# Edge loop of a graph network: three engines issue in text order, and a dense unit's result stands ahead of the next unit's first transposes

## The chip, the cores and the metric

The kernel runs on one core of one Trainium2 chip. A core has a matrix engine (PE, with its weight loads PEld), a vector engine (DVE), a scalar engine (ACT), a general engine (POOL) that here issues the indirect gathers, and a queue engine (SP) that issues the other transfers. Each engine takes its instructions in the order in which the program hands them over, and waits on semaphores for the others. Sixteen DMA engines serve the core. The metric is device time in microseconds for one execution; a single core runs, so its time is the time.

## The reference

Two graph networks follow each other over the same 3125 nodes and 100,000 edges (`src`, `dst`, sorted by `dst` in the drawn inputs). The first has four layers of attention over the incoming edges of a node, with 8 heads of 16:

```python
q = (h @ Wq.T + bq)[dst].reshape(-1, HEADS, D_HEAD)
k = (h @ Wk.T + bk)[src].reshape(-1, HEADS, D_HEAD)
v = (h @ Wv.T + bv)[src].reshape(-1, HEADS, D_HEAD)
alpha = jnp.sum(q * k, axis=-1) / float(np.sqrt(D_HEAD))
amax = jax.ops.segment_max(alpha, dst, num_segments=n)
ex = jnp.exp(alpha - amax[dst])
denom = jax.ops.segment_sum(ex, dst, num_segments=n)
a = ex / (denom[dst] + 1e-16)
out = jax.ops.segment_sum((a[:, :, None] * v).reshape(-1, f), dst, num_segments=n)
...
beta = jax.nn.sigmoid(jnp.concatenate([out, x_r, out - x_r], axis=-1) @ Wbeta.T)
return beta * x_r + (1.0 - beta) * out
```

After each attention come a layer norm and a two-layer GELU network with residuals. The second network sums one message per edge into its node and updates the nodes; the change does not touch it.

## The kernel before

Edges are sorted by target and cut into chunks of 128 that stay within one tile of 128 nodes. A group `g` is 4 chunks (512 edges). Nodes of the first 4 tiles (`DT`) have so many edges that their attention is done densely, as a matrix over all nodes with a mask of edge counts; the other nodes' edges go through the edge loop in 123 groups (`SPG`). So one layer runs two things interleaved in one loop, `edge_sums`.

**Edge steps.** `rows_of(g)` gathers the group's k and v rows into one of 5 `kvg` buffers (4 indirect DMAs, issued by POOL, L690). `fetch` loads (layers 1 to 3) the one-hot rows that layer 0 built and stored; `one_hot` builds them in layer 0 (L674). `select` multiplies them on PE with q (L754, `q_ps`, two buffers). `scores` multiplies by k and reduces to `alpha` on DVE (L766, L767). `values` copies v out of `kvg` on ACT (L776). `weights` scales v by the exponentials on DVE (L793) and, in layer 0, builds one-hot columns (L681). `by_node` sums over a node's edges on PE (L808, `s_ps`, one buffer until the last 8 groups), and `add` adds that to the accumulators on DVE (L824).

**Turns.** Turn `g` of the loop runs, in the text, `rows_of(g+4)`, `fetch(g+3)`, `add(g-14)`, `one_hot(g+2)`, dense slots, one step of `mixing` if due, `scores(g)`, `select(g+1)`, `advance()`, dense slots, `values(g)`, `advance()`, `columns(g-11)`, `weights(g-12)`, `advance()`, `by_node(g-13)`. `LAG` is 12: the exponentials need the maxima of a batch of 8 groups (`GB`). From turn -3 to 136, a layer has 140 turns.

**Maxima.** `Maxima.steps` is a generator that takes one batch's `alpha` through transposes on PE (`m_ps`, L585, L564, L554, L634), copies and scans on DVE (L591, L566, L594 to L598, L557, L600, L604, L612, L614, L618) and copies and exponentials on ACT (L587, L628 to L638). Each `advance()` runs it up to its next `yield`; the first three pieces fall into the turn of the batch's last group, b=7, the next three into the turn after. Pieces 3 to 6 each end with a PE transpose of what DVE has just made in the same piece:

```python
yield from self.row(top[:, 0:1], back[:, :, :IB])
```

**Dense steps.** `dense_steps` cuts the dense attention into 16 units (4 tiles, 4 pairs of heads) and 258 slots of 15 a unit; `due(at, count, step)` places a step of unit `u` in the slots from `15u + at` on. A unit computes scores chunk by chunk (`scores`, L897, `d_ps`, one buffer), adds the mask and takes the maximum on DVE (`masked`, L907), takes exponentials on ACT (`exps`, L920, 14 of them), transposes on PE into `pt_ps`, one buffer (`turn`, L929), copies that out on ACT (`turned`, L936), and multiplies by v on PE (`weigh`, L946, `av`). After every fourth unit `result` copies `av` out (L951), transposes it through `pt_ps` (L954) and adds two halves on ACT and DVE (L959, L960). `others` runs 14 slots in the first turn and then 1.92 slots a turn. Within a slot the text has `weigh`, `scores`, `turned`, `exps`, `turn`, `masked`, `maxima`, `result`.

**What sets the order.** In the kernel before, the program's framework orders the instructions of every engine itself: it walks a model of their times and takes those whose inputs are there, the earlier in the text first. Buffers of a pool go round in the order of the text, and a new user waits until the last one has been read.

**Mixing.** When a block of 4 node tiles is complete, 9 steps of `mixing` (L1100 to L1146) are popped one a turn, four blocks a layer.

Of the kernel before, what the change touches and what calls it, by code (L numbers as in the profile page):

```python
# [14 lines left out]
ET = mybir.EngineType  # L15
# [851 lines left out]
PAIRS = [(0, 2), (1, 3), (4, 6), (5, 7)]  # L867
# [3 lines left out]
def dense_steps(tc, k, s, a, keep, work, ps):  # L871

    nc = tc.nc
    v, kt, qz = a["v"], a["kt"], a["qz"]
    chunks = [(c, min(NS, NT - c)) for c in range(0, NT, NS)]
    units = [(d, pair) for d in range(DT) for pair in PAIRS]
    live = {}  # L880
    dense = keep.tile([P, DT, HEADS, DX], F32, name="dense")

    av = ps.tile([P, len(PAIRS), P], F32, name="av", bufs=1)
    nc.vector.memset(av, 0.0)

    def scores(u, j):
        d, pair = units[u]
        c, n = chunks[j]
        if j == 0:
            live[u] = dict(mx=work.tile([P, 2, len(chunks)], F32, name="mx"), sm=[], s_ps={},  # L890
                           t_ps={}, pt={})
        mask = work.tile([P, NS * P], F32, name="mask", bufs=2)
        nc.sync.dma_start(mask[:, :n * P], s["mask_d"][d, :, c * P:(c + n) * P])
        s_ps = [ps.tile([P, NS * P], F32, name=f"d_ps{i}", bufs=1) for i in range(2)]
        for i, h in enumerate(pair):
            r = slice(h // 2 * 32, h // 2 * 32 + 32)
            nc.tensor.matmul(s_ps[i][:, :n * P], qz[r, h % 2, d * P:(d + 1) * P],  # L897
                             kt[r, c * P:(c + n) * P], start=True, stop=True)
        live[u]["s_ps"][j] = s_ps, mask

    def masked(u, j):
        n = chunks[j][1]
        s_ps, mask = live[u]["s_ps"].pop(j)
        sm = work.tile([P, 2, NS * P], F32, name="sm", bufs=9)
        live[u]["sm"].append(sm)
        for i in range(2):
            nc.vector.tensor_tensor_reduce(  # L907
                out=sm[:, i, :n * P], in0=s_ps[i][:, :n * P], in1=mask[:, :n * P], scale=1.0,
                scalar=-3.0e38, op0=ALU.add, op1=ALU.max, accum_out=live[u]["mx"][:, i, j:j + 1])

    def maxima(u):
        top = work.tile([P, 2], F32, name="dtop")
        nc.vector.tensor_reduce(top, live[u]["mx"], axis=AX.X, op=ALU.max)
        nc.vector.tensor_scalar(top, top, -1e20, -1.0 / DH ** 0.5, op0=ALU.max, op1=ALU.mult)  # L914
        live[u]["top"] = top

    def exps(u, j, i):
        n = chunks[j][1]
        sm = live[u]["sm"][j]
        nc.scalar.activation(sm[:, i, :n * P], sm[:, i, :n * P], AF.Exp,  # L920
                             scale=1.0 / DH ** 0.5, bias=live[u]["top"][:, i:i + 1])

    def turn(u, i):
        t_ps = ps.tile([P, 2, 2, P], F32, name="pt_ps", bufs=1)
        for x in range(min(2, NT - 2 * i)):
            t = 2 * i + x
            sm = live[u]["sm"][t // NS]
            for y in range(2):
                nc.tensor.transpose(t_ps[:, x, y, :], sm[:, y, t % NS * P:(t % NS + 1) * P],  # L929
                                    k.ident)  # L930
        live[u]["t_ps"][i] = t_ps

    def turned(u, i):
        n = min(2, NT - 2 * i)
        pt = work.tile([P, 2, 2, P], F32, name="pt")
        nc.scalar.copy(pt[:, :n], live[u]["t_ps"].pop(i)[:, :n])  # L936
        live[u]["pt"][i] = pt

    def weigh(u, i):
        d, pair = units[u]  # L940
        pt = live[u]["pt"].pop(i)
        for x in range(min(2, NT - 2 * i)):
            t = 2 * i + x
            for y, h in enumerate(pair):
                r = (2 * x + y) * 32
                nc.tensor.matmul(av[r:r + DX, u % len(PAIRS), :], v[:, t, h, :], pt[:, x, y, :],  # L946
                                 start=(i == 0), stop=(t + 2 >= NT))

    def result(d):
        out = work.tile([P, len(PAIRS), P], F32, name="dout", bufs=1)  # L950
        nc.scalar.copy(out, av)  # L951
        t_ps = ps.tile([P, len(PAIRS), 2, 2, 32], F32, name="pt_ps", bufs=1)
        for j in range(len(PAIRS)):
            nc.tensor.transpose(t_ps[:, j].rearrange("p x y d -> p (x y d)"), out[:, j, :],  # L954
                                k.ident)

        o = dense[:, d].rearrange("p (a y b) d -> p a b y d", a=2, b=2)
        for a_ in range(2):
            nc.scalar.copy(o[:, a_], t_ps[:, 2 * a_:2 * a_ + 2, 0, :, :DX])  # L959
            nc.vector.tensor_add(o[:, a_], o[:, a_], t_ps[:, 2 * a_:2 * a_ + 2, 1, :, :DX])  # L960

    NH = (NT + 1) // 2
    NC_ = len(chunks)

    def slot(i):

        def due(at, count, step):

            u, j = divmod(i - at, 15)
            if 0 <= u < len(units) and j < count:  # L970
                step(u, j)

        due(19, NH, weigh)
        due(0, 2 * NC_, lambda u, j: scores(u, j // 2) if j % 2 == 0 else None)
        due(18, NH, turned)
        due(15, 2 * NC_, lambda u, j: exps(u, j // 2, j % 2))
        due(17, NH, turn)
        due(1, 2 * NC_, lambda u, j: masked(u, j // 2) if j % 2 == 0 else None)
        due(14, 1, lambda u, j: maxima(u))
        due(19 + NH, 1, lambda u, j: result(units[u][0]) if u % len(PAIRS) == len(PAIRS) - 1  # L980
            else None)
        due(19 + NH, 1, lambda u, j: live.pop(u))

    return dense, [lambda i=i: slot(i) for i in range(15 * (len(units) - 1) + 20 + NH)]


# [169 lines left out]
def attention(tc, k, s, a, l):  # L1156


    nc = tc.nc
    nc.gpsimd.memset(a["acc"], 0.0)  # L1160

    def pools(name, groups, dense):
        with tc.tile_pool(name=name + "k", bufs=1) as keep, \
                tc.tile_pool(name=name + "w", bufs=2) as work, \
                tc.tile_pool(name=name + "m", bufs=1) as mw, \
                tc.tile_pool(name=name + "p", bufs=1, space=PSUM) as ps:
            if dense:

                early = [(upto * IC // GC + LAG + 2, step) for b, upto in DONE.items()
                         for step in mixing(tc, l, a, mw, b)]  # L1170
                sums, beside = dense_steps(tc, k, s, a, keep, work, ps)
                edge_sums(tc, k, s, a, groups, beside, early, "load" if l else "store", keep,
                          work, ps, ps)

                nc.vector.tensor_copy(a["acc"][:, :DT], sums)
            else:
                edge_sums(tc, k, s, a, groups, [], [(groups + LAG + 2, step) for b in DONE
                                                    for step in mixing(tc, l, a, mw, b)],
                          None, keep, work, ps, ps)

    with tc.If(s["general"] == 0) as arm:
        pools("some", SPG, True)
    with arm.Else():
        pools("all", NG, False)
# [597 lines left out]
```

## Time and profile before

| What | us |
|---|---|
| runs | 4689.97, 4687.6, 4693.14 (median 4689.97) |
| the profiled execution | 4700.52 |
| its span, first to last instruction | 4698.7 |
| edge loop of layer 0 | 350 to 1112 |
| edge loop of layer 1 | 1206 to 1913 |
| edge loop of layer 2 | 2009 to 2718 |
| edge loop of layer 3 | 2812 to 3523 |
| second network | about 3600 to the end |

In the page, the 40 slices show the loops as the stretches in which PE, DVE and POOL are all high:

```profile
PE   3757999887799989879989888998987666667775
DVE  5765989986478888548878854887875444445643
...
POOL 2014777760477776047777514777742777777775
PEclk9666989898789999969999996999998888888887
```

Each digit is a tenth of busy time in a slice of 117 us, the last row the granted clock of PE. A group's line in the page names the source line, the engine, the tiles it writes and reads, its count, its busy time and mean, and then the idle time of the engine just before it and what ended most of that:

```profile
L936 ACT COPY pt<-pt_ps 128x512 f32<-128x512 f32 (+1 forms) x832 | 471.4, 567 | 804.0 <-PE pt_ps L929 796.5
L920 ACT ACTIVATE sm<-sm,dtop 128x512 f32<-128x512 f32 (+1 forms) x896 | 539.8, 668 | 14.9 <-DVE dtop L914 14.1
```

ACT has much idle time; an instruction there is seldom late for want of the engine, but those behind a long run of others wait for it.

### The profile page before, as it was taken

What the parts mean: (1) busy time and instruction counts of PE and PEld (TensorE: products, weight loads), DVE (VectorE), ACT (ScalarE), POOL (GpSimd) and SP (SyncE); (2) the same over time, 40 slices, a digit from 0 to 9 for tenths busy, and PEclk for the clock granted to TensorE, in tenths of its full rate; (3) what the DMA queues carried; (4) which work ended last, traced back from release to release, by engine and by line L of the source; (5) the groups of instructions that cost most, each with busy time, mean ns of one, the idle gap of its engine ahead of it and who ended that gap; (6) DMA issues with size and microseconds to landing.
All of it is one profiled execution on the core that took longest, in us unless ns stands there. A gap on an engine that the chain in (4) does not pass through costs nothing. (4 is left out here: it accounts for less than half of the span.)

```text
span 4698.7 us, 84645 instructions
## 1 busy us (share of the span) xinstructions
PE 3820.5 (81%) x25947; PEld 2695.1 (57%) x25947; DVE 3205.5 (68%) x9975; ACT 2183.8 (46%) x4470; POOL 2808.9 (60%) x2821
## 2 busy tenths in 40 slices
PE   3757999887799989879989888998987666667775
PEld 1324666664466666546666644666664665656664
DVE  5765989986478888548878854887875444445643
ACT  2873555454256555535555543555544323332331
POOL 2014777760477776047777514777742777777775
PEclk9666989898789999969999996999998888888887
DMA  2125888882578778357877735787862333334332
GB/s 58 40 96 174 270 251 266 243 230 76 180 218 261 246 242 226 98 167 242 261 240 247 193 113 173 245 262 231 253 178 60 93 93 90 91 90 87 97 90 52
DMA packets 449718, 801.31 MB, mean 171 GB/s; under 512 B 91381, under 2 KB 173830, under 8 KB 449184
## 3 DMA queue, kind: packets, MB, share of 16 engines
q1 hardware_dynamic: 327040, 481.12, 31.7%
q0 software_dynamic: 121392, 313.35, 25.6%
q8 instruction: 229, 3.75, 0.3%
q14 instruction: 273, 2.24, 0.2%
q10 hardware_dynamic: 784, 0.85, 0.1%
HBM read 693.94 MB, written 102.26 MB: 169 GB/s over the span
## 5 line engine op out<-in xcount | busy, mean ns | idle before, releaser
L690 POOL DMA_INDIRECT kvg<-kv_d,src_i x1968 | 1967.7, 1000 | 1086.3 <-issue 620.1
L690 POOL DMA_INDIRECT ag<-a_d,src_i x816 | 794.5, 974 | 255.3 <-issue 222.7
L936 ACT COPY pt<-pt_ps 128x512 f32<-128x512 f32 (+1 forms) x832 | 471.4, 567 | 804.0 <-PE pt_ps L929 796.5
L907 DVE CUSTOM_DVE_ANT_0 sm<-d_ps,mask 128x512 f32<-128x512 f32 (+1 forms) x896 | 542.1, 625 | 230.5 <-PE d_ps L897 132.3
L897 PE MATMUL d_ps<-kt,qz 32*128 32x512 f32 (+1 forms) x1792 | 603.2, 659 | 47.9 <-DVE mx L907 42.0
L929 PE MATMUL pt_ps<-ident,sm 128*128 128x128 f32 x3200 | 572.4, 301 | 74.5 <-ACT pt L936 48.1
L754 PE MATMUL q_ps<-q,hrows 128*128 x3936 | 611.0, 301 | 12.1 <-issue 6.5
L929 PEld LDWEIGHTS pt_ps<-ident,sm 128*128 128x128 f32 x3200 | 366.5, 149 | 401.1 <-issue 207.2
L754 PEld LDWEIGHTS q_ps<-q,hrows 128*128 128x128 f32 x3936 | 543.0, 212 | 88.7 <-issue 63.5
L808 PE MATMUL s_ps<-ev,hcols 128*128 128x136 f32 x3744 | 567.4, 295 | 16.4 <-DVE acc L824 7.6
L920 ACT ACTIVATE sm<-sm,dtop 128x512 f32<-128x512 f32 (+1 forms) x896 | 539.8, 668 | 14.9 <-DVE dtop L914 14.1
L808 PEld LDWEIGHTS s_ps<-ev,hcols 128*128 128x128 f32 x3744 | 500.2, 200 | 45.2 <-issue 23.7
L776 ACT COPY ev<-kvg 128x512 f32<-128x512 f32 x492 | 302.7, 617 | 439.7 <-DMA kvg<-kv_d,src_i 260.5
L1567 PE MATMUL s_ps<-m,hcols 128*128 128x129 f32 x1632 | 278.1, 323 | 258.4 <-DVE acc L1576 236.7
L1567 PEld LDWEIGHTS s_ps<-m,hcols 128*128 128x128 f32 x1632 | 248.0, 230 | 294.6 <-ACT m L1560 166.2
L1559 DVE TENSOR_TENSOR m<-ag,m_ps 128x512 f32<-128x512 f32 x204 | 139.7, 687 | 393.5 <-DMA ag<-a_d,src_i 353.9
L766 DVE TENSOR_TENSOR qk<-q_ps,kvg 128x512 f32<-128x512 f32 x492 | 336.1, 683 | 100.8 <-PE q_ps L754 88.0
L946 PE MATMUL av<-pt,v 128*17 128x128 f32 x6400 | 367.5, 286 | 0.7 <-ACT pt L936 0.7
L793 DVE TENSOR_TENSOR ev<-ev,ex 128x512 f32<-128x512 f32 x492 | 333.3, 682 | 7.5 <-ACT ex L638 7.2
L767 DVE TENSOR_REDUCE alpha<-qk 128x32 f32<-128x512 f32 x492 | 333.0, 677 | 3.2
L1560 ACT ACTIVATE m<-m 128x512 f32<-128x512 f32 x204 | 125.1, 627 | 436.4 <-DVE m L1559 430.7
L824 DVE TENSOR_TENSOR acc<-acc,s_ps 128x136 f32 x936 | 266.8, 285 | 40.1 <-PE s_ps L808 31.5
(324 smaller groups left out, 5180.1 us busy)
## 6 DMA issues: line engine op xcount, KB each, us to landing
mask<-mask_d SPq DMA_DIRECT2D x384, 256.0 KB
hrows<-hrows_d SPq DMA_DIRECT2D x369, 256.0 KB
hcols<-hcols_d SPq DMA_DIRECT2D x369, 256.0 KB
hrow<-drow_d SPq DMA_DIRECT2D x327, 128.0 KB
kvg<-kv_d,src_i POOLq DMA_INDIRECT x1968
hrows_d<-hrows SPq DMA_DIRECT2D x123, 256.0 KB
hcols_d<-hcols SPq DMA_DIRECT2D x123, 256.0 KB
ag<-a_d,src_i POOLq DMA_INDIRECT x816
```

Source lines behind the costliest of these rows:

```text
L690: nc.gpsimd.indirect_dma_start(out=out[:, x, :], out_offset=None, in_=table[:], in_offset=bass.IndirectOffsetOnAxis(ap=s["src_i"][:, i:i + ...
L754: nc.tensor.matmul(qs[g][:, x, :], hot[:, c * P:(c + 1) * P], a["q"][:, bass.ds(tn["PE"][item_of(g, c)], 1), :], start=True, stop=True)
L766: nc.vector.tensor_mul(qk, qs.pop(g), kvg[:, :, :HID])
L793: nc.vector.tensor_mul(e[:, :, :, :DH], e[:, :, :, :DH], ex.unsqueeze(3).to_broadcast([P, IC, GH, DH]))
L808: nc.tensor.matmul(sums[g][:, c // IC], hot[:, c, :], ev[:, ORDER.index(c)].rearrange("p h d -> p (h d)"), start=(c % IC == 0), stop=(c % ...
L897: nc.tensor.matmul(s_ps[i][:, :n * P], qz[r, h % 2, d * P:(d + 1) * P], kt[r, c * P:(c + n) * P], start=True, stop=True)
L907: nc.vector.tensor_tensor_reduce(out=sm[:, i, :n * P], in0=s_ps[i][:, :n * P], in1=mask[:, :n * P], scale=1.0, scalar=-3.0e38, op0=ALU.add ...
L920: nc.scalar.activation(sm[:, i, :n * P], sm[:, i, :n * P], AF.Exp, scale=1.0 / DH ** 0.5, bias=live[u]["top"][:, i:i + 1])
L929: nc.tensor.transpose(t_ps[:, x, y, :], sm[:, y, t % NS * P:(t % NS + 1) * P], k.ident)
L936: nc.scalar.copy(pt[:, :n], live[u]["t_ps"].pop(i)[:, :n])
L946: nc.tensor.matmul(av[r:r + DX, u % len(PAIRS), :], v[:, t, h, :], pt[:, x, y, :], start=(i == 0), stop=(t + 2 >= NT))
L1567: nc.tensor.matmul(s_ps[:, c // IC, :], h[:, c, :], x[:, c, :], start=(c % IC == 0), stop=(c % IC == IC - 1))
```

## The change

Two edits. The edge loop is wrapped so that PE, ACT and DVE keep the order of the text; POOL and SP are still ordered by the framework. And in a slot, `result` now stands before `turn`.

```diff
@@ dense_steps, slot
         due(15, 2 * NC_, lambda u, j: exps(u, j // 2, j % 2))
+        due(19 + NH, 1, lambda u, j: result(units[u][0]) if u % len(PAIRS) == len(PAIRS) - 1
+            else None)
         due(17, NH, turn)
         due(1, 2 * NC_, lambda u, j: masked(u, j // 2) if j % 2 == 0 else None)
         due(14, 1, lambda u, j: maxima(u))
-        due(19 + NH, 1, lambda u, j: result(units[u][0]) if u % len(PAIRS) == len(PAIRS) - 1
-            else None)
         due(19 + NH, 1, lambda u, j: live.pop(u))
@@ attention, pools
                 sums, beside = dense_steps(tc, k, s, a, keep, work, ps)
-                edge_sums(tc, k, s, a, groups, beside, early, "load" if l else "store", keep,
-                          work, ps, ps)
+
+                with tc.manual_schedule(engines={ET.PE, ET.Activation, ET.DVE}):
+                    edge_sums(tc, k, s, a, groups, beside, early, "load" if l else "store", keep,
+                              work, ps, ps)
```

`result` of unit `u` falls into slot 15u + 32, which is also the slot of the first `turn` of unit `u + 1`; both use the one buffer of `pt_ps`. In the text before, `turn(u+1, 0)` would take that buffer first and its copy, `turned(u+1, 0)`, comes in the next slot, behind `result`. In the new text `result` writes and frees it before `turn` does. No instruction is added or taken away.

## The prediction

> **What bounds the kernel now.** First the page's span and engine rows, then the busy time by stage, then the timelines of single batches.
>
> ```profile
> span 4698.7 us, 84645 instructions
> PE 3820.5 (81%) x25947; PEld 2695.1 (57%) x25947; DVE 3205.5 (68%) x9975; ACT 2183.8 (46%) x4470; POOL 2808.9 (60%) x2821
> L690 POOL DMA_INDIRECT kvg<-kv_d,src_i x1968 | 1967.7, 1000 | 1086.3 <-issue 620.1
> ```
>
> The change touches the four edge loops (first d_ps product to last addition: 350 to 1112, 1206 to 1913, 2009 to 2718, 2812 to 3523), 2888 of the 4699 us. The busy time by stage of layer 1 (columns: stretch, length, then busy time and instructions of PE, PEld, DVE, ACT, POOL, granted clock, DMA share, GB/s); the last row is the same part of layer 0.
>
> ```profile
> 1219.00:1283.50 64.50, 49.65 (x228) 28.05 (x227) 24.48 (x66) 19.99 (x34) 29.18 (x31) 0.62 0.50 153
> 1328.30:1861.50 533.20, 496.37 (x4159) 350.56 (x4159) 447.66 (x1323) 300.06 (x644) 406.37 (x412) 0.96 0.80 247
> 1413.80:1451.00 37.20, 36.57 (x321) 26.06 (x321) 32.81 (x93) 22.94 (x51) 28.36 (x30) 1.00 0.84 265
> 1565.00:1613.10 48.10, 41.26 (x323) 29.06 (x321) 33.77 (x93) 24.69 (x54) 36.52 (x39) 0.89 0.73 230
> 427.20:1044.70 617.50, 561.34 (x4454) 391.03 (x4454) 558.41 (x1595) 325.10 (x694) 468.46 (x446) 0.91 0.83 251
> ```
>
> Row 2 is the steady part, turns 15 to 119: 13 batches of 8 turns, 41.0 us each. PE is busy 93%. POOL has a floor: a gather takes 0.95 us and the next follows 0.30 later, so the 32 of a batch need 40.0 us. Little is left to win there: (41.0-40.0) x 13 = 13 us a layer. Row 3 is a good batch: PE has no gap and the clock is full. Row 4 is a bad one, and the timelines of PE and ACT show why:
>
> ```profile
> 1567.23 0.39 PE L946 MATMUL av<-pt,v 128*17 128x128 f32 x2
> 1574.46 0.37 PE L564 MATMUL m_ps<-ident,fwd 128*1 128x128 f32 x1 [6.84 <-DVE fwd L591]
> 1575.31 2.08 PE L754 MATMUL q_ps<-q,hrows 128*128 x8
> ```
> ```profile
> 1567.24 6.20 ACT L920 ACTIVATE sm<-sm,dtop 128x512 f32<-128x512 f32 x11
> 1573.34 0.35 ACT L587 COPY at<-m_ps 128x256 f32<-128x256 f32 x1
> ```
>
> ACT was given 11 exponentials of a dense unit ahead of the copy that the edge maxima wait for; PE stood for 6.84 us and then ran at half clock (2.08 for a q product of 1.06). By the waits of PE in row 2's stretch, L564 waits for DVE fwd 28.0 us in 9 waits. Over the batches of layers 1 to 3, length minus PE gaps minus half of the half-clock time is 35 to 40, mean 36.6 us: PE's own work.
>
> **The change, part by part.** Nothing is added or removed but order: PE, ACT and DVE now follow the text; SP and POOL don't. Outside the maxima turns PE's order is already the text's (av, d, T, q, av, T, s; starts 0.35, 1.06, 0.49, 0.99, 0.35, 0.49, 1.02 us apart), so a plain turn costs the same. Three things change.
>
> (a) *The exponentials are spread, one a slot.* The 6.8 us gap and its like go. Cleared of gaps and slow clock a batch is 36.6.
>
> (b) *PE now waits at the maxima steps.* In turns b=7, +1 and +2 of every batch, advance() puts a DVE step and the PE transpose that needs it side by side, five times; the trace moves those transposes behind the next s, av and d, the text doesn't. DVE's turn starts when PE ends the turn before (add needs the last s_ps). DVE steps, start to start: two adds 0.65, qk+alpha 1.32, a masked pair 1.25, ev 0.61, forward scan 0.66, backward 0.65, small copies and scan 0.90. Walk from a turn's start at 0, scores in the first slot. Turn b=7: alpha is done at 2.0, PE's alpha transpose goes at 2.9 unhindered; DVE's masked pair and ev end at 3.9, ACT's copy at 4.1, fwd at 4.8; PE arrived at 4.05: 0.95 lost. Next turn: rows are ready at 2.9, PE there at 2.9: 0.2 with the hand-over; then masked, col, fwd, back to 5.55, PE there at 4.1: 1.6; then ev, copy, scan, copy to 6.95, PE there at 6.0: 1.15. Third turn: sub at 3.2, gains, ACT's exponential at 4.35, PE there at 3.73: 0.8. Sum 4.7. With scores in the second slot the masked pair comes before qk: 1.6 + 2.5 + 0.85 + 1.5 = 6.45. Parity flips at every 15-slot unit: mean 5.5 us a batch (4 to 8). Behind the waiting transpose stand s, av, d and T on PE, and DVE's next add and ACT's next pt copy wait for those. The 28 mixing steps a layer (1.4 to 2 us of DVE) fall for 3/8 into these turns: 28 x 3/8 x 1.6 = 17, over 14 batches 1.0 with a little for the others (0 to 1.6).
>
> Half clock after gaps: in layer 1 a gap of 2.06 us at 1826.89 was followed by d, T, q of 1.40, 1.11, 1.92 (granted clock 0.67 over 4 us), one of 2.35 at 1747.75 by none (1.00). New gaps are 0.2 to 2.5 us; I take 0.8 us a batch (0 to 3). [...]
>
> Steady batch: 36.6 + 5.5 + 1.0 + 0.8 = 43.9 against 41.0: +2.9 x 13 = +38 us a layer. POOL (40) isn't the bound then. Layer 0 computes one-hots: hot_rows and hot_cols add 0.9 us of DVE to each maxima turn, some 1.2 of it seen by PE a batch. 37.2 (same way) + 6.7 + 1.0 + 0.8 = 45.7 against (1044.7-472.0)/13 = 44.0 (starts of the q products of turns 119 and 15): +22.
>
> (c) *The start.* From the first d_ps product (1206.5) to the q product of turn 15 (1328.3) it takes 121.8 us; row 1 shows PE at clock 0.62. ACT ran 13 exponentials in a row (1250.80, 7.75 us), T waited 5.8 and 4.0, by its timeline POOL stood 28 us more than in its rhythm from 1222 to 1300. In the text all 7 chunks of unit 0 come first: first masked pair ends at 1214.9 as now, then six rounds of 2.08 (cold d) + 1.31 + 0.2, the last short: 1235. Then turns without s_ps: two cold ones of 6, eleven of 3.7, two of 4.7, one batch of maxima with 7.6: about 1304. Gain 24 us (5 to 35), all layers.
>
> (d) *The dense result ahead of turn.* turn(u+1,0) shares pt_ps, one buffer: PE now waits for dout (0.58, behind one exponential of 0.67), four transposes (0.61), two copies and two additions of 0.2 with hand-overs, before its T: 2.3 us (0 to 3.5), 4 a layer: +9. It issues no DMA; behind it stand T, q or s on PE and the masked pair on DVE, which it now precedes. Before, T was already issued and s covered the transposes (1424.59).
>
> (e) *Tail*, turn 119 to the last addition, 51.5 us now: ten turns of add, ev, s of 1.6, the rest as above: +2 (-5 to +8). SP's and POOL's own order may shift; PE waited 0.6 us for hrows in row 2's stretch, so I take 0.
>
> Layers 1 to 3: 38-24+9+2 = +25 each, 75; layer 0: 22-24+9+2 = +9. **Sum +84**. The profiled execution took 4700.5 us (span 4698.7): 4784.5, 1.8% more. Against the median 4690.0: **4774 us**.
>
> **Rivals.** *The covers hold (faster).* If PE reaches each transpose late enough (as in the good batch), or DVE runs ahead, batches stay at 41.0, result costs nothing, the start's 24 us are won: -22 x 4 = -88, 4602; with all batches at POOL's 40.0 (DVE's busy time in layer 0, 558.4/14 = 39.9, allows it) (13+24) x 3 + (52+24) = 187 less, 4503. For: row 3, and the bursts of exponentials surely go. Against: the walk finds PE early at five steps.
>
> *Half clock in every batch (slower still).* If the new gaps put PE at half clock for most of each maxima stretch, 3 us more a batch, so 46.9: layers 1 to 3 +64 each, layer 0 +48, total +240: 4930. For: the start stays at 0.62 with gaps of only 0.4 to 0.8 us between 1225 and 1243. Against: the 2.35 us gap left 1.00. It decides from gaps of about 2 us in each 3 to 4 us window.
>
> *Nothing happens.* The order is the text's in most turns already; gains at the start and losses in the batches cancel: within 10 us of 4690. This is just +64 in the batches eaten by a better start.
>
> **Chances.** Forecast 0.50 (own range 4705 to 4860), faster 0.25, half clock 0.17, nothing 0.08. The range 4605 to 4910 leaves out half of the faster case and somewhat over half of the half-clock one, 0.2 in all. A measurement of this kernel tells about 0.2% (9 us) from no change: faster 0.25, same 0.08, slower 0.67.
>
> **What would show it.** Right: no run of more than 3 exponentials on ACT in a row; waits of L564, L554 and L634 on PE of 0.5 to 2.5 us, four or five a batch, some 75 us a layer where row 2 had 34; the start over 20 us shorter; L954 followed by a wait of about 2 us at T. Wrong: batches of 41 or less, PE gaps under 3 us a batch, or POOL at its 1.25 us rhythm without a break: then the text hides the round trips and it is faster. Clock under 0.9 in the steady part: the half-clock case.

## The result, and the profile after

| | before | after |
|---|---|---|
| median, us | 4688.78 (4685.03 to 4693.14) | 5023.46 (5017.87 to 5034.8) |
| ratio to before, 95% interval | | 1.0718 (1.07 to 1.0736) |
| profiled execution, us | 4700.52 | 5022.12 |
| its span, us | 4698.7 | 5020.3 |

The change makes the kernel 7.2% slower. The direction was forecast, the size was not: +84 us of span were predicted and +322 came, beyond the forecast's 4605 to 4910.

The page after, first its span, the busy time of the engines and PE's granted clock in 40 slices, then one group (busy time, mean ns of one, idle time before it and what ended most of it):

```profile
span 5020.3 us, 84716 instructions
...
PE 3931.7 (78%) x25947; PEld 2802.8 (56%) x25947; DVE 3369.9 (67%) x9975; ACT 2156.9 (43%) x4470; POOL 2794.8 (56%) x2821
...
PEclk7658888887888888888888888888888788888887
...
L824 DVE TENSOR_TENSOR acc<-acc,s_ps 128x136 f32 x936 | 276.4, 295 | 479.5 <-PE s_ps L808 455.1
```

The counts of PE and DVE are those of before, and yet PE was busy 111 us longer with them: the same instructions ran more slowly, at a mean granted clock of 0.830 (0.871 before). (DVE's 164 us more were not followed up.) The clock row had nines in the four loops before; now it stays at 8. The last line is new among the costly ones. In the page of before it reads:

```profile
L824 DVE TENSOR_TENSOR acc<-acc,s_ps 128x136 f32 x936 | 266.8, 285 | 40.1 <-PE s_ps L808 31.5
```

DVE's first step of a turn, the addition, now waits 455 us for PE's last step of the turn before; it used to wait 31.5. PE and DVE go in lockstep.

Stages of the kernel after, from the busy time by stretch (length, then PE, PEld, DVE, ACT, POOL with instructions, granted clock, DMA share, GB/s). In order: steady part of layer 1 (turns 15 to 119), one batch of it, steady part of layer 0, start of layer 1, its tail:

```profile
1394.20:2020.40 626.20, 536.66 (x4160) 380.36 (x4159) 474.57 (x1316) 292.95 (x642) 417.69 (x424) 0.86 0.70 213
1532.40:1578.20 45.80, 40.44 (x327) 28.78 (x327) 34.60 (x94) 22.39 (x50) 31.93 (x33) 0.89 0.75 224
...
444.80:1128.10 683.30, 558.54 (x4159) 394.31 (x4158) 575.53 (x1523) 293.71 (x642) 426.83 (x417) 0.85 0.72 214
1306.10:1394.20 88.10, 75.64 (x502) 45.77 (x502) 54.26 (x141) 39.45 (x72) 50.20 (x53) 0.81 0.72 220
2020.40:2087.00 66.60, 45.09 (x332) 35.13 (x330) 47.26 (x147) 22.36 (x60) 2.99 (x4) 0.82 0.38 80
```

A steady batch took 626.2 / 13 = 48.2 us where it took 41.0. The start of the layer is indeed shorter (121.8 us before), and its clock is 0.81 where the start before had 0.66 (0.62 in the stretch that the prediction shows).

Cut in the same way, every layer says the same. *Start* runs from the first d_ps product to the q product of turn 15, *steady* from there to that of turn 119, *tail* to the last addition. *Gaps* are the idle stretches of PE over 0.1 us in the steady part, *half clock* the time in it for which the trace grants PE about half its clock.

| us | start | steady | tail | gaps | half clock |
|---|---|---|---|---|---|
| before, layer 0 | 121.5 | 572.7 | 67.1 | 51.2 | 85.3 |
| before, layer 1 | 121.8 | 533.2 | 51.1 | 36.6 | 44.4 |
| before, layer 2 | 121.7 | 533.3 | 54.2 | 37.7 | 41.0 |
| before, layer 3 | 121.9 | 537.1 | 51.8 | 39.8 | 44.4 |
| after, layer 0 | 97.3 | 683.3 | 84.7 | 124.7 | 211.6 |
| after, layer 1 | 88.2 | 626.2 | 66.7 | 89.3 | 177.5 |
| after, layer 2 | 88.1 | 625.5 | 67.0 | 89.8 | 174.1 |
| after, layer 3 | 88.7 | 628.9 | 66.8 | 87.6 | 187.7 |

The four loops grew by 104, 75, 71 and 74 us, 324 in all: the whole difference of the spans (322).

The waits of PE in the steady part of layer 1 (waiting line, releaser: us in total, times, longest):

```profile
PE m_ps L554 <- DVE rows L598: 26.8, 13, 4.9
PE m_ps L554 <- DVE into L614: 18.0, 13, 1.5
PE m_ps L564 <- DVE back L609: 12.2, 7, 2.2
PE m_ps L585 <- DVE alpha L767: 8.4, 5, 3.1
PE m_ps L564 <- DVE fwd L591: 7.0, 8, 1.4
PE m_ps L634 <- ACT at L628: 3.5, 6, 1.7
```

Two of these, `rows` and `into`, occur 13 times, once in every batch. The maxima transposes are the places, as the walk said. L554, L564 and L634 come to 70 us with the smaller rows, where "some 75 us a layer" had been forecast; L585 adds 8. One second maxima turn, on PE and then on DVE (start, duration, and in brackets the idle time before and what ended it):

```profile
1490.23 1.16 PE L754 MATMUL q_ps<-q,hrows 128*128 x8
1492.12 0.19 PE L554 MATMUL m_ps<-ident,into 1*128 1x1 f32 x1 [0.73 <-DVE rows L598]
1492.24 0.40 PE L946 MATMUL av<-pt,v 128*17 128x128 f32 x4
1494.85 0.37 PE L564 MATMUL m_ps<-ident,top 128*1 128x128 f32 x1 [2.21 <-DVE back L609]
1496.59 0.23 PE L554 MATMUL m_ps<-ident,into 1*128 1x1 f32 x1 [1.36 <-DVE into L614]
1496.75 2.18 PE L808 MATMUL s_ps<-ev,hcols 128*128 128x136 f32 x8
1498.86 2.08 PE L897 MATMUL d_ps<-kt,qz 32*128 32x512 f32 x4
```

```profile
1488.94 0.63 DVE L824 TENSOR_TENSOR acc<-acc,s_ps 128x136 f32 x2 [1.29 <-PE s_ps L808]
...
1496.18 0.26 DVE L614 COPY into<-back 1x120 f32<-1x120 f32 x1
1498.97 0.63 DVE L824 TENSOR_TENSOR acc<-acc,s_ps 128x136 f32 x2 [2.53 <-PE s_ps L808]
1502.27 0.23 DVE L960 TENSOR_TENSOR dense<-dense,pt_ps 128x68 f32<-128x68 f32 x1 [2.67 <-ACT dense L959]
```

The walk had 0.2, 1.6 and 1.15 us for these three waits of PE; they were 0.73, 2.21 and 1.36. After them the products s and d take 2.18 and 2.08 us at a granted clock of 0.50 (1.09 and 1.13 at 1.00, from 1535.37 on), and DVE's next addition waits 2.53 us for that slow s. Behind the gaps stands a second loss, at half clock, and DVE passes it into the next turn, which begins with that addition.

### The profile page after: what moved, and what is told of

It reads as the page before. It is cut to its first block, busy times and chain, and to the rows that moved or that the text cites. A ratio compares the mean times of both kernels' runs of the same rounds, so it can differ in the third digit from the quotient of the medians.

```text
span 5020.3 us, 84716 instructions
## 1 busy us (share of the span) xinstructions
PE 3931.7 (78%) x25947; PEld 2802.8 (56%) x25947; DVE 3369.9 (67%) x9975; ACT 2156.9 (43%) x4470; POOL 2794.8 (56%) x2821
## 5 line engine op out<-in xcount | busy, mean ns | idle before, releaser
L920 ACT ACTIVATE sm<-sm,dtop 128x512 f32<-128x512 f32 (+1 forms) x896 | 600.8, 677 | 114.1 <-DVE dtop L914 114.1
L808 PE MATMUL s_ps<-ev,hcols 128*128 128x136 f32 x3744 | 625.3, 319 | 10.2 <-DVE bs L1135 3.1
L897 PE MATMUL d_ps<-kt,qz 32*128 32x512 f32 (+1 forms) x1792 | 589.3, 701 | 38.6 <-DVE mx L907 32.6
L754 PE MATMUL q_ps<-q,hrows 128*128 x3936 | 600.8, 303 | 21.9 <-DVE acc L824 3.5
L929 PE MATMUL pt_ps<-ident,sm 128*128 128x128 f32 x3200 | 588.8, 310 | 31.1 <-ACT pt L936 17.2
L929 PEld LDWEIGHTS pt_ps<-ident,sm 128*128 128x128 f32 x3200 | 380.7, 154 | 395.1 <-issue 251.7
L907 DVE CUSTOM_DVE_ANT_0 sm<-d_ps,mask 128x512 f32<-128x512 f32 (+1 forms) x896 | 528.3, 626 | 91.7 <-PE d_ps L897 64.9
L808 PEld LDWEIGHTS s_ps<-ev,hcols 128*128 128x128 f32 x3744 | 556.8, 222 | 26.8 <-issue 13.1
```

The source lines that it names most:

```text
L754: nc.tensor.matmul(qs[g][:, x, :], hot[:, c * P:(c + 1) * P], a["q"][:, bass.ds(tn["PE"][item_of(g, c)], 1), :], start=True, stop=True)
L808: nc.tensor.matmul(sums[g][:, c // IC], hot[:, c, :], ev[:, ORDER.index(c)].rearrange("p h d -> p (h d)"), start=(c % IC == 0), stop=(c % ...
L907: nc.vector.tensor_tensor_reduce(out=sm[:, i, :n * P], in0=s_ps[i][:, :n * P], in1=mask[:, :n * P], scale=1.0, scalar=-3.0e38, op0=ALU.add ...
```

## The experiments

All ratios are to before. The start, steady and tail times and the gaps are read as in the table. For each kernel that keeps the text order, the comparison is with after.

**The result's move alone.** The text order is taken away.

```diff
-                with tc.manual_schedule(engines={ET.PE, ET.Activation, ET.DVE}):
+                if True:
```

> Only the moved result; the three engines are ordered by the framework as before. If the order of the text is the whole cause, this is the kernel before again: 4680 to 4700 us (ratio 0.998 to 1.003), steady batches of layer 1 at 41 us, clock 0.96 there. If the result ahead of turn costs the 2.3 us each that the prediction gave it, 16 of them add up to 37 us: 4725.

4699.5 us, ratio 1.0005 (0.999 to 1.0019). The move by itself costs nothing that can be measured; layer 1 has 36.1 us of gaps and 51.2 of half clock, near before's 36.6 and 44.4. All of the 7.2% comes with the text order.

**ACT alone in the order of the text.**

```diff
-                with tc.manual_schedule(engines={ET.PE, ET.Activation, ET.DVE}):
+                with tc.manual_schedule(engines={ET.Activation}):
```

> Only ACT keeps the order of the text; PE and DVE are ordered by the framework. If the runs of 11 to 13 exponentials on ACT are what cost the kernel before its long PE gaps, they go and nothing else gets worse: no wait of PE for fwd over 3 us, steady batches at 38 to 40 us, 4560 to 4640. If pacing ACT costs as much elsewhere (PE waits for pt copies that stand behind a late exponential), 4680 to 4760.

4682.8 us, ratio 0.9963 (0.9947 to 0.9979): slightly faster, and less so than expected. The starts are 11 to 20 us shorter, the steady parts of layers 1 to 3 gain 9.5, 3.0 and 6.2 us, and the tails lose 12 to 18; layer 0's steady part lost 9.4. The long waits did shrink: PE's wait for `fwd` in the steady part of layer 1 fell from 28.0 to 13.8 us. But spreading the exponentials is worth little in the batches, because they then meet the gathers: layer 1's batch is 523.7 / 13 = 40.3 us, next to the 40.0 that its 32 gathers take, and DVE's waits for gathered rows rose from 5.0 to 26.6 us.

**Filler ahead of every wait.** In the transposes of the maxima, further transposes of the identity go into the same buffer ahead of the real one; the result of the computation is the same.

```diff
@@ column (row: the same with 4)
-        col_ps = self.ps.tile([P, 1], F32, name="m_ps")
+        full = self.ps.tile([P, P], F32, name="m_ps")
+        for _ in range(5):
+            nc.tensor.transpose(full, self.k.ident, self.k.ident)
+        col_ps = full[:, 0:1]
```

> The changed kernel with filler: ahead of each maxima transpose of a row PE does 4, of a column 5 transposes of the identity into the same buffer, overwritten by the real one; nothing waits for less. Theory (half clock): the waits were 6.5 us a batch, the other half of the loss was PE at half clock behind them. The filler keeps the clock up: granted clock in the steady part of layer 1 from 0.86 to 0.94 or more, batches from 48 to 42 to 45 us, the time 4750 to 4900. Rival (the clock is a symptom; DVE sets the pace of these turns and PE is never late): clock up, time unchanged within 0.5%, 5000 to 5050, or longer by the filler's own 5 us a batch, up to 5280.

5020.1 us, ratio 1.0685 (1.0657 to 1.0712): the time hardly moved. The clock of the steady part of layer 1 did rise, from 0.86 to 0.91 where 0.94 was expected, and its half-clock time fell from 177.5 to 109.2 us. One reason for the shortfall shows in the trace: the filler does not fill the wait. It goes into the one m_ps buffer, so its first transpose has itself to wait until DVE has copied the last result out (2.20 us in the rows below); 25.9 us of PE's gaps in the steady part of layer 1 end at such a filler in L555. By the total alone the run speaks for the rival, that the clock costs nothing, but the filler takes PE's time as well. One batch of this kernel tells the clock from everything else. Its busy time by stretch in layers 1, 2 and 3:

```profile
1574.15:1617.31 43.16, 38.35 (x335) 27.56 (x335) 35.73 (x100) 21.57 (x48) 30.88 (x32) 1.00 0.78 230
2444.51:2487.69 43.18, 38.36 (x335) 27.56 (x335) 35.83 (x100) 21.63 (x48) 31.17 (x31) 1.00 0.76 232
3324.34:3371.41 47.07, 42.36 (x334) 30.37 (x335) 35.70 (x98) 21.59 (x48) 30.39 (x31) 0.89 0.70 211
```

The same instructions in the same order take 43.2 us twice and 47.1 us once. DVE, ACT and POOL are busy the same time; PE is not, and only its clock differs. PE in the first and in the third of them (start, duration, idle time before and releaser; L555 is the filler, L557 the transpose behind it, L903 the d product):

```profile
1582.41 0.74 PE L555 MATMUL m_ps<-ident 128*128 128x128 f32 x5 [2.20 <-DVE rows L572]
1583.09 0.22 PE L557 MATMUL m_ps<-ident,into 1*128 1x1 f32 x1
1583.09 1.13 PE L903 MATMUL d_ps<-kt,qz 32*128 32x512 f32 x4
...
3332.62 1.30 PE L555 MATMUL m_ps<-ident 128*128 128x128 f32 x5 [2.20 <-DVE rows L572]
3333.85 0.26 PE L557 MATMUL m_ps<-ident,into 1*128 1x1 f32 x1
3333.85 2.08 PE L903 MATMUL d_ps<-kt,qz 32*128 32x512 f32 x4
```

The gap is 2.20 us in both. Behind one of them PE goes on at full clock, behind the other at half, for 10.2 us by the clock records. That cost 47.07 - 43.17 = 3.9 us, or 0.38 us for each us of half clock.

In the trace the two differ in their place among the clock records. These say 1.00 or 0.50, and all of them, 354 in the trace of after and 254 in that of before, start within 0.01 us of a grid of 3.41 us. Here are the two slices of this grid that the first gap lies in, and then the two from the third batch:

```profile
1577.99:1581.40 3.41, 2.22 (x19) 1.69 (x18) 2.50 (x8) 0.19 (x2) 2.55 (x3) 1.00 0.65 203
1581.40:1584.81 3.41, 2.40 (x16) 1.49 (x17) 2.99 (x8) 0.00 (x0) 2.50 (x4) 1.00 0.85 264
...
3329.03:3332.44 3.41, 1.39 (x12) 0.99 (x11) 3.33 (x9) 0.00 (x0) 2.68 (x3) 1.00 0.69 196
3332.44:3335.85 3.41, 3.23 (x10) 1.43 (x10) 2.39 (x9) 0.00 (x0) 2.61 (x3) 0.50 0.75 258
```

The first gap is cut in two by the grid, 1.19 and 1.01 us, and both slices and the next are at 1.00; of the other, 2.02 us fall into one slice, where PE is busy for 1.39 of 3.41 us, and the next slice has 0.50. The two gaps that the prediction compares part in the same way: of the 2.06 us, 1.91 lie in one slice, and the next one is at half clock, while the 2.35 us are cut into 1.08 and 1.27. In these four cases half clock went with the idle time in one slice and not with the length of the gap. In the four steady parts of after, 73 slices at full clock had 1.7 us of idle time or more, and 70 of them were followed by half clock; of the 452 with less, 8 were. In before it is 23 of 23 and 7 of 544. These are counts of what stood together; no run set the idle time of a slice by itself.

The price can be had from more batches as well. A fit over the 195 steady batches of layers 1 to 3 of five kernels (after and the four that differ from it by filler or by mixing), each compared with the same batch of the other layers at equal gaps, gives 0.39.

**The round trips pulled apart.** The generator yields once more before each transpose, so that DVE's step and the PE transpose that needs it no longer stand side by side; a fourth `advance()` keeps the number of turns near what it was.

```diff
@@ column and row
         nc = self.tc.nc
+        yield
@@ turn
         others(at_once + per_turn * max(0, g + 0.5))
+        advance()
```

> The changed kernel with one more break in the maxima steps: a transpose on PE is issued one advance() after the DVE step it needs, and a turn has four advances, the new one between the first dense slots and scores. Theory (PE waits because step and transpose stand side by side): PE's waits for L554 and L564 fall from 66 us a layer to under 25, clock to 0.93 or more, batches of 41 to 43 us, 4650 to 4780. Rival (DVE is late by a whole turn, because its first instruction waits for PE's last product of the turn before, so one advance more is not enough): waits above 45 us a layer, 4900 to 5050.

4760.3 us, ratio 1.0127 (1.0102 to 1.0151). Of the 7.2 per cent, 5.9 are gone. PE's waits for DVE at the two transposes, in the steady part of layer 1 of this kernel (its lines stand one or two later than before's):

```profile
PE m_ps L555 <- DVE into L616: 11.3, 10, 3.0
PE m_ps L555 <- DVE rows L600: 7.8, 7, 2.4
PE m_ps L555 <- DVE into L599: 5.1, 3, 2.6
...
PE m_ps L566 <- DVE back L611: 3.8, 6, 2.0
```

These are 28 us; at the same two transposes after had some 66. The gaps fell from 89.3 to 57.0 us, the half clock from 177.5 to 81.9. With the price above that makes 32.3 + 95.6 x 0.38 = 69 us; the steady part shortened by 58.4, so the account is 10 us too generous here. DVE's wait for s_ps fell too, from 108.1 to 64.9 us.

**Filler at two of the transposes only.** As in the first filler kernel, but the number of fillers is an argument, zero by default.

```diff
@@ Maxima.steps
-        yield from self.row(top[:, 0:1], back[:, :, :IB])
+        yield from self.row(top[:, 0:1], back[:, :, :IB], 5)
...
-        col = yield from self.column(self.into[1])
+        col = yield from self.column(self.into[1], 4)
```

> As the filler run, but filler (5 and 4 transposes of the identity) stands only ahead of the second row and the second column transpose of a batch, where PE waited longest in the changed kernel (about 2.2 and 1.4 us), so that nearly all of it lies in time that PE stood. Theory (the half clock behind the waits costs some 4 us a batch by itself): half-clock time in the steady part of layer 1 from 177 to 80 us or less, 2 to 4 us less a batch, the time 4860 to 4960. Rival (DVE sets the pace of these turns, PE's speed there doesn't count): less half-clock time, the time within 0.5% of the changed kernel's 5023.

5040.2 us, ratio 1.0725 (1.0697 to 1.0754). The filler did not hold the clock: layer 1 still has 157.0 us at half (177.5 in after). Here too the filler waits for its buffer, and PE's largest wait, 28.2 us for `rows` at the first column transpose, has no filler at all. The run decides nothing about the clock's share.

**Additions later in the turn.**

```diff
@@ turn
-        at(g - LAG - 2, add)
...
         at(g - LAG, weights)
+        at(g - LAG - 2, add)
         advance()
```

> The changed kernel with add(g-14) moved in the text from the head of a turn to behind weights(g-12), so that DVE's first instruction of a turn no longer waits for PE's last product of the turn before. Theory that the lockstep of DVE with PE's turn end makes the maxima steps late: DVE's wait for s_ps (108 us in the steady part of layer 1) falls under 60, PE's waits for L554 and L564 from 66 to 30 to 45 us a layer, 4780 to 4920. Rival (the round trips themselves are too long, whenever DVE starts): within 1% of 5023.

4889.5 us, ratio 1.0397 (1.0364 to 1.043). Of the 7.2 per cent, 3.2 are gone. DVE's wait for s_ps, 108 us in after, is no longer among its waits; PE's waits at the two transposes fell from 66 to 52 us, less than the 30 to 45 expected. The move has a price of its own, though. Three rows of this kernel in the steady part of layer 1, two of PE and one of DVE:

```profile
PE m_ps L554 <- DVE into L614: 22.5, 12, 2.0
PE s_ps L808 <- DVE acc L824: 13.1, 20, 2.1
```

```profile
DVE sm L907 <- PE d_ps L897: 60.3, 56, 2.8
```

PE now waits 13.1 us for the one s_ps buffer, which the late addition frees late, and DVE 60.3 us for the next d product.

**Mixing steps away from the maxima turns.**

```diff
@@ turn
-        if early and early[0][0] <= g:
+        if early and early[0][0] <= g and (1 < g % GB < GB - 1 or g >= ng):
```

> The changed kernel with the mixing steps kept out of the three maxima turns (they are popped only in turns with g % 8 from 2 to 6, or after the last group). The batches with mixing are 5 to 13 us longer in the changed kernel (54.5, 49.4, 49.8, 50.8, 59.5 us against 45 to 48). Theory (DVE steps of 1.4 to 2 us standing ahead of scores are paid in full in a maxima turn and little elsewhere): batches with mixing fall to 46 to 49 us, 20 to 30 us less a layer, 4910 to 4950. Rival (mixing costs the same wherever it stands): within 0.5% of 5023.

5035.1 us, ratio 1.0712 (1.0685 to 1.074), as after. In the total, where the mixing stands makes no difference that can be told: the steady parts of layers 1 to 3 are 4 to 11 us shorter, the starts and tails together 3 to 7 us longer.

**The three together** (split, late additions, mixing apart).

> The text order with three moves together: the split maxima steps with four advances a turn, add behind weights, mixing outside the maxima turns. Theory that these three waits are what the order of the text costs: steady batches of layer 1 at 39 to 41 us, POOL near its 1.25 us rhythm, start as in the changed kernel (30 us shorter than before), the time 4520 to 4640, faster than the kernel before. Rival (the order of the text has further waits of its own): 4690 to 4760.

4752.9 us, ratio 1.012 (1.0093 to 1.0147), about what the split alone gave. The steady part of layer 1 is 565.6 us, 32 more than before: 61.4 - 36.6 = 24.8 us of gaps and (64.9 - 44.4) x 0.38 = 7.8 of half clock. The largest of PE's waits there is a new one:

```profile
PE s_ps L810 <- DVE acc L826: 39.7, 47, 2.1
```

It is the wait for the one s_ps buffer that the late additions bring, 13.1 us when they were moved alone and none in before, and it is more than all that the gaps have grown. So the move that ends the lockstep costs about what it wins once the round trips are apart. What the text order would cost without the lockstep and without this wait was not tried.

**PE and ACT in text order, DVE not.**

```diff
-                with tc.manual_schedule(engines={ET.PE, ET.Activation, ET.DVE}):
+                with tc.manual_schedule(engines={ET.PE, ET.Activation}):
```

> The changed kernel with DVE ordered by the framework, PE and ACT in text order. If what costs is that DVE's steps stand late in DVE's own text (behind add, qk, masked, ev), DVE moves the maxima steps ahead and PE's waits shrink: L554 and L564 under 35 us in the steady part of layer 1, 4720 to 4850. If it is the place of the transposes in PE's text, whatever DVE does: over 55 us, 4950 to 5050.

4815.7 us, ratio 1.0262 (1.0245 to 1.0279). PE still waits some 63 us at the two transposes in the steady part of layer 1, as the second case has it, but the time is that of the first: half clock is 102.4 us and DVE's wait for s_ps is 18.6 us instead of 108.1. A PE that keeps the text waits for the round trips whatever orders DVE; with DVE free they cost less. That this is the lockstep's absence is likely, not shown.

**DVE alone in text order.**

```diff
-                with tc.manual_schedule(engines={ET.PE, ET.Activation, ET.DVE}):
+                with tc.manual_schedule(engines={ET.DVE}):
```

> Only DVE keeps the order of the text; PE and ACT are the framework's, so the transposes can be moved behind other products again. If the place of the transposes in PE's text is the cost, the batches are near the kernel before: 4680 to 4780. If DVE's lockstep (108 us of waiting for s_ps) is the cost by itself: 4850 to 5000.

4855.9 us, ratio 1.0341 (1.0324 to 1.0358). Waits of PE at the two transposes and of DVE for s_ps in the steady part of layer 1 of this kernel:

```profile
PE m_ps L554 <- DVE into L614: 3.9, 7, 1.0
...
PE m_ps L564 <- DVE back L609: 2.2, 5, 0.9
```

```profile
DVE acc L824 <- PE s_ps L808: 47.8, 44, 4.1
```

Here the framework moves PE's transposes behind other products, and their waits for DVE shrink to some 10 us. DVE's lockstep remains with 47.8 us (6.7 in before), and DVE's text order costs 3.4% by itself. How it does so is shown in part only: more gaps (46.7 us) and half clock (61.4) make 10.1 + 6.5 = 17 of the 32 us by which the steady part grew. The two losses, of PE and ACT in text order and of DVE, add up to 6.0%, near the 7.2% of all three.

**Filler where PE waits for nothing.** Eighteen transposes of the identity a batch, six at the end of each of turns 3, 4 and 5 of it; the result is the same.

```diff
@@ turn
         at(g - LAG - 1, by_node)
+        if kept is not None and GB < g < ng and 3 <= g % GB <= 5:
+            full = pm.tile([P, P], F32, name="m_ps")
+            for _ in range(6):
+                nc.tensor.transpose(full, k.ident, k.ident)
```

> Control to the filler run e3: the changed kernel with the same 18 transposes of the identity a batch (some 5 us of PE), but 6 each at the end of the turns with g % 8 = 3, 4 and 5, where PE doesn't wait, so they fill no gap and help no clock. e3 took 5020 us with half-clock time down from 177 to 109 us a layer. If PE's speed counts and the filler was paid for by the clock in e3: here half-clock time stays at 165 to 190, the steady part grows by 30 to 65 us a layer, the time 5140 to 5280. If the filler costs nothing because PE has slack (POOL or DVE sets the pace): 5010 to 5060, and then the clock was not worth anything in e3.

5104.1 us, ratio 1.0864 (1.0839 to 1.0889), 81 us above after. A batch got about 18 x 0.12 = 2.2 us of PE's work, and the steady part of layer 1 grew by 17.9 us, 1.4 a batch, although its half clock fell by 17 us. The filler is smaller than was expected, but PE's time counts even where PE is idle 14% of the stretch. That gives the first filler kernel its account: its 18 fillers a batch keep PE busy for 43 us in the steady part of layer 1 (23.4 at L555, 20.1 at L568, some of it at half clock), gaps are -16, half clock -68.3 x 0.38 = -26. The sum is +1; it was -2.4. So the unmoved total can be read as a cancellation. This is an account, no separate proof.

**The text order in the head alone.** The loop's body becomes a function; turns -3 to 7 are in text order on the three engines, the rest is ordered as before (the move of `result` stays).

```diff
-    for g in turns:
+    def one_turn(g):
...
+    for lo, hi, engines in [(-3, 8, {ET.PE, ET.Activation, ET.DVE}), (8, 999, None)]:
+        text = kept is not None and engines
+        with tc.manual_schedule(engines=engines) if text else nullcontext():
+            for g in turns:
+                if lo <= g < hi:
+                    one_turn(g)
```

> The three engines keep the order of the text only in turns -3 to 7 of each layer's loop; from turn 8 on the framework orders them as in the kernel before. The changed kernel's start was 33 us a layer shorter in layers 1 to 3 and 24 in layer 0, its batches 92 us a layer longer. Theory (the gain is in the start, the loss in the batches, and they are apart): start 88 to 98 us, steady part 530 to 545, total 4690 - 90 to 125: 4565 to 4600. Rival (the lead that the short start wins is given back, since POOL's rhythm binds the rest): 4660 to 4700.

4640.8 us, ratio 0.9888 (0.9872 to 0.9905). Faster than before, and short of what was expected: the starts are 12 to 14 us shorter, not 33, presumably because turns 8 to 14 are ordered as before again; the next kernel bears this out.

**The same head, then ACT alone in text order up to turn 115** (the diff is against the kernel above).

```diff
-    for lo, hi, engines in [(-3, 8, {ET.PE, ET.Activation, ET.DVE}), (8, 999, None)]:
+    for lo, hi, engines in [(-3, 8, {ET.PE, ET.Activation, ET.DVE}), (8, 116, {ET.Activation}), (116, 999, None)]:
```

> As e9, and ACT alone keeps the order of the text in turns 8 to 115; the last turns are the framework's. ACT in text order alone gave 2 to 9 us a layer in the steady part and lost 18 in the tail. Theory (both are won, the tail's loss comes from ACT's last turns): tail 51 to 55 us, 4540 to 4590. Rival (the tail's loss has another cause): tail 65 to 70, 4600 to 4650.

4618.3 us, ratio 0.9844 (0.9825 to 0.9863): 1.6% faster than before and 0.5% faster than the last, by more than the measurement's doubt. The time lies in the rival's range, the tail (58.0 us) in neither. Its page:

```profile
span 4618.0 us, 84771 instructions
...
PEclk9667999988899998989999989999988888888887
```

Layer 1 has a start of 94.0 us, a steady part of 536.9 and a tail of 58.0: most of the start's gain is kept (121.8 before, 88.2 after), the batches are at before's 533.2 within 4 us, and nines have come back to the clock row. It is not that both gains add up: against the last kernel the starts win 16 to 18 us a layer, but the steady parts lose 8 to 11 and the tails of layers 1 to 3 some 5.

## Why the prediction was right in direction and wrong in size

The span grew by 322 us where the sum had 84, so 238 are missing.

**Where it failed.** The step is the term of half clock: "New gaps are 0.2 to 2.5 us; I take 0.8 us a batch (0 to 3)." The gaps came as described, and no more of them: in layer 1 89.3 / 13 = 6.9 us a batch against 5.5 + 1.0 = 6.5. But behind them PE was at half clock in every batch, 177.5 / 13 = 13.7 us of it, at 0.38 us each 5.2 us. So the term was mis-sized by 4.4 us a batch, and the others of the batch close: 48.2 - 6.9 - 5.2 = 36.1 for PE's own work, where 36.6 was taken. Over 13 batches and by each layer's own half clock that is 57, 56 and 61 us in layers 1 to 3 and 70 in layer 0 (211.6 x 0.38 / 13 = 6.2 against 0.8), 244 together: as much as the whole miss. That the rest nearly cancels is luck: the starts came 29 us better than forecast and the cost of `result` (36) hardly showed, but the tails came 53 worse and the rest of the batches 8. The share is derived from equal batches of one kernel and from the fit; no run removed the half clock and nothing else.

The evidence had been in the text. Of two gaps in before, 2.06 us had brought half clock and 2.35 had not, and the low value was taken from the second. What parts the two in the trace is their place on the grid (1.91 us of the first in one slice, 1.08 and 1.27 of the second), and the turn above has three gaps, 4.3 us within 5.2. The slice from 1490.82 to 1494.23 holds the first and most of the second: PE is busy for 1.09 of its 3.41 us, 2.32 are idle, and the 13.65 us behind it are at 0.50. No batch in the steady parts of after has less than 3.4 us of half clock. The forecast's own rival, "half clock in every batch", came near: its condition, "gaps of about 2 us in each 3 to 4 us window", agrees with the counts (70 of 73 slices of 3.41 us with 1.7 us or more), and it had 46.9 us for a batch, against 48.2 measured. It was given 0.17.

**The other steps.**

| step | predicted, us | measured, us |
|---|---|---|
| steady batch, layer 1: gaps | 6.5 | 6.9 |
| steady batch, layer 1: half clock | 0.8 | 5.2 |
| steady batch, layer 0: gaps | 7.7 | 9.6 |
| start, layers 1 to 3 | -24 each | -33.6, -33.6, -33.2 |
| start, layer 0 | -24 | -24.2 |
| tail, layers 1 to 3 | +2 each | +15.6, +12.8, +15.0 |
| tail, layer 0 | +2 | +17.6 |
| result, a layer | +9 | 0 by itself; 2.3 of wait on PE in text order |

(a) The exponentials are spread: ACT has no run of more than two of them in layer 1 after. Right, and worth little in the batches, as ACT alone showed, where the gathers were the next bound.

(b) The walk's places and their sum were right. That mixing steps matter more in the maxima turns was not borne out: moving them away did not change the total. (The 17 us for them over 14 batches are 1.2 a batch, not the 1.0 that was used.) That DVE's turn starts when PE ends the turn before was used for the walk, but its price was not seen: DVE's text order costs 3.4% alone, with some 10 us of wait for DVE at the transposes.

(c) The start was right in sign and too small. PE's gaps in it fell from 24.4 to 12.5 us in layer 1 and the half clock from 81.9 to 34.1; by the price 0.38 that is 11.9 + 18.2 = 30 of the 33.6.

(d) The wait at the next unit's transposes is there, but small on PE: L929 waits 2.3 us for `dense` in 2 waits a layer. DVE takes the larger one, 11.2 us at L960, behind ACT's L959 (above, 2.67 us; 0.9 in before). Without the text order the move costs nothing. How much of its cost in the text order is the move's was not tried.

(e) The tail was taken as even, but it holds maxima turns too: in layer 1 PE waits 8.9 us in it at L554 and L564, its gaps grew from 11.5 to 21.6 us and its half clock from 10.2 to 23.9. That is 10.1 + 5.2 = 15 of the 15.6. The steady terms should have run to the end of the layer. Pulling the round trips apart brings the tail down to 58.6. But layer 1's tail grows whichever engine keeps the text: 69.3 us with ACT alone, 62.4 with DVE alone, 59.2 with PE and ACT, and 58.0 in the last kernel, whose ACT is free from turn 116 on. So it is not one engine's doing, and how the shares combine stays open.

**The rivals.** That the covers hold fell: PE was early at `rows` and `into` in every batch, and 12 of layer 1's 13 batches took 43.9 us or more, so POOL's 40.0 was not the bound. That nothing happens fell with it, though the start's gain it counted on is real and can be had with little of the loss, as the last kernel shows.

## What to carry to other kernels

Before a matmul engine is bound to the order of the text, look for pairs where another engine's short step and the matmul that needs it stand side by side: here the three in the turn shown cost PE 0.73, 2.21 and 1.36 us, and to the 6.9 us of gaps a batch the half clock added some 5.2, an estimate from its 13.7 us a batch at 0.38. A text that yields between the two halves of such a pair gives most of the loss back (7.2% became 1.3% here), and one that binds only the stretch in which the scheduler does badly (here the first turns of a layer) keeps a gain (1.1%, and 1.6% with ACT bound longer). Price a gap not by its length alone but with the half clock that may follow, and sum the gaps that fall close together: in after's steady parts half clock followed 70 of 73 slices of 3.41 us with 1.7 us or more of them, and 8 of 452 with less.

## What the runs showed of the hardware

Half clock came in pieces of 3.41 us and multiples of it: in the steady parts of after 11 of 3.41 us, 21 of 6.83, 27 of 10.24, 14 of 13.65 and 5 of 20.48. The same gap of 2.20 us in the same instructions of the first filler kernel brought 10.2 us of it in one layer and none in two others. What differed in the two batches read slice by slice was PE's idle time in one slice of the grid of 3.41 us on which the clock records lie: 2.02 us against 1.19 and 1.01. With 1.7 us of it or more in a slice at full clock, the next slice was at half 70 of 73 times in after and 23 of 23 in before; with less, 8 of 452 and 7 of 544. In the first filler kernel the counts part less sharply: 50 of 50 with 1.7 us or more, but also 25 of 533 with less. In the steady parts of after, full clock came back 78 times, each time behind a slice with 0.62 us of idle time or less. PE at half clock for one us made the batch 0.38 to 0.39 us longer, where the prediction's 36.6 had taken off 0.5. Why it is less is open; that waits take part of it up does not show in the pair of equal batches, where PE's busy time grew by 4.0 us and the batch by 3.9. Small transposes of 128x128 f32 back to back cost some 0.12 us each at full clock (in the first filler kernel five up to the next start in 0.68 us, four in 0.44).
